# A recommender forward pass: the order of the last block, and a bias term fed through the contraction

## The chip, the cores and the metric

The kernel runs on one core of a Trainium2 chip. The metric is the device time of one execution in microseconds, shown as the median of three runs. A core has a matrix engine (TensorE, "PE" in the profile; its weight loads are shown as "PEld"), a vector engine (VectorE, "DVE"), a scalar engine (ScalarE, "ACT"), GpSimd ("POOL") and a sync engine (SyncE, "SP"). Each works through its own instructions in their order, and they wait for one another through semaphores. Data is worked on in SBUF (128 partitions); matmuls write into PSUM. Transfers from device memory are issued from an engine's queue; indirect ones (gathers by index) are issued by GpSimd, one instruction for 128 rows.

## The reference

For each of 16384 samples there are 69 user fields and one label, all of them indices into one table of 100001 rows of 96 floats. Every field's row `u` is weighed by an attention value from a small net on `[q, u, q - u, q * u]`, where `q` is the label's row; the weighed rows are summed in ten groups, and a three-layer net runs on the ten sums and `q`. Everything is float32.

```python
u = emb[batch_user]                              # (B, 69, 96)
ql = emb[batch_label[:, 0]]
z = concatenate([q, u, q - u, q * u], axis=-1)   # q: ql for each field
h = dice(z @ W1 + b1, a1)                        # 384 -> 64
att = (h @ W2 + b2) @ W3 + b3                    # 64 -> 16 -> 1
pre = where(batch_user < ITEM_NUM, u * att, 0)
x = concatenate([einsum('gf,bfe->bge', window, pre), ql])
h = dice(bn(x @ Wf1 + bf1), af1)                 # 1056 -> 200
h = dice(bn(h @ Wf2 + bf2), af2)                 # 200 -> 80
return h @ Wf3 + bf3
```

`dice(x, a)` is `(a * (1 - p) + p) * x` with `p = sigmoid(x)`. The groups hold 20, 20, 10, 10, 2, 2, 2, 1, 1 and 1 fields.

## The kernel before

**Tiling.** Samples come in 32 blocks of 512 (`BLK`). A block's 69 x 512 rows are cut into 69 chunks of 512 rows: 64 main chunks, each of 8 samples times the first 64 fields, and 5 single-field chunks, each one of the last five fields for all 512 samples. Two chunks make a pair `i`; there are 1104 pairs. `chunk(c)` (L232) says which chunk stands at place `c`; in the last block it puts the five single-field chunks after three quarters of the main ones.

**A pair's way.** `fetch(i)` (L299) issues eight gathers of 128 rows into `u` and turns each with a PE transpose into PSUM (`ptr`). From a half of it DVE makes `quT` (the rows times `q`) and then ACT `uT` (a copy). With `A = W1[1] - W1[2]`, `C = W1[0] + W1[2]`, and `Wp = W1[3]`, the first layer is `A.T uT + Wp.T quT + c`, where `c` (q through `C`, plus `b1`) is the same for all fields of a sample. `head_row(n)` (L252) makes `c` of a block. `seed(i)` (L276) opens the accumulation in PSUM with a bf16 matmul of zeros and lets ACT copy `c` into it, spread over the fields. `hidden(i)` (L323) adds the two products, each chunk into its own 64 of the 128 output partitions, and makes `y` by a sigmoid and a linear step on ACT and a product on DVE. `attend_rows` (L334) takes the attention values of four pairs, `spread` (L350) turns them and multiplies the group windows in (`rw`), and `pool(i)` (L367) sums a pair's rows into `pooled` with eight matmuls into the PSUM tile `acc` and a DVE copy. Single-field chunks go through `attend_tail` (L343) into `pres`. An fp32 matmul stands in the trace as two records, each with its weight load; these are called passes.

**Top net.** `top1` (L404), `top2` and `top3` run on a block's `pooled`, `qTs` and `pres`; `top_steps` (L439) cuts it into ten steps: eight quarter-parts of the two output halves of the first layer (together 16 matmuls for a half), then `top2`, then `top3`. `top3` writes each block's results out by an own transfer. `tail_weights` (L217) makes, early on, the weights of the single-field chunks on DVE.

**Order.** The order is written out by hand: the kernel turns the framework's scheduler off, and the loop at L481 puts, in step `i`, the stages of different pairs one behind the other: `seed(i-1)`, `pool(i-8)` (`POOL_LAG`), a band's `attend_rows`, `attend_tail(i-3)`, a band's `spread`, `hidden(i-2)`, `fetch(i)`, and then what `plan` holds for the step. That is the order in which each engine's queue gets its instructions. In the last fetching step four pools more are put ahead of the fetch (L503). The last block's top net runs in two halves of the samples, the first beside the last pairs, the second after the last pool.

**Buffers.** `u` has 14, `uT` and `quT` five, `y` eight; the indices of a block (`ids`) two. PSUM has two buffers each for transposes, `ph` and the small tiles, one for `acc` and one for the top net (`ps_m`).

**Start.** `ids` of block 0 is the first transfer on SP's queue; about twenty small transfers of weights follow on SP's and ACT's queues (L114 to L182).

Of the kernel before, what the change touches and what calls it, by code (L numbers as in the profile page):

```python
# [30 lines left out]
BF16 = mybir.dt.bfloat16  # L32
# [5 lines left out]
P = 128  # L38
# [6 lines left out]
BLK = 512  # L45
# [16 lines left out]
EARLY = 3 * NMAIN // 4  # L62
# [3 lines left out]
def rec_kernel(  # L66
# [5 lines left out]
    W1: bass.AP,  # L72
    b1: bass.AP,
    a1: bass.AP,
    W2T: bass.AP,
    b2: bass.AP,
    W3: bass.AP,
    b3: bass.AP,
    Wf1: bass.AP,
    bf1: bass.AP,  # L80
    af1: bass.AP,
    Wf2: bass.AP,
    bf2: bass.AP,
    af2: bass.AP,
    Wf3: bass.AP,
    bf3: bass.AP,
    wrow: bass.AP,
    wtile: bass.AP,
# [7 lines left out]
    tpool = ctx.enter_context(tc.tile_pool(name="tpool", bufs=5))  # L96
    hpool = ctx.enter_context(tc.tile_pool(name="hpool", bufs=3))
    ypool = ctx.enter_context(tc.tile_pool(name="ypool", bufs=8))
# [3 lines left out]

    def load_ids(n):
        ids = ipool.tile([P, NCOL], I32, tag="ids", name=f"ids{n}")
        nc.sync.dma_start(out=ids, in_=idx[n : n + 1].rearrange("o p n -> (o p) n"))
        return ids

    ids = {0: load_ids(0)}

# [4 lines left out]
    w1 = const.tile([E, 4, H1], F32, name="w1")  # L114
    nc.sync.dma_start(out=w1, in_=W1.rearrange("(k e) h -> e k h", e=E))
    Cq = const.tile([E + 1, 2, H1], F32, name="Cq")
    for i in range(2):
        nc.vector.tensor_add(Cq[0:E, i, :], w1[:, 0, :], w1[:, 2, :])
    nc.sync.dma_start(
        out=Cq[E : E + 1], in_=b1.rearrange("(o q h) -> o q h", o=1, q=1).to_broadcast([1, 2, H1])  # L120
    )
    Wp = w1[:, 3, :]
    A = const.tile([E, H1], F32, name="A")
    nc.vector.tensor_sub(A, w1[:, 1, :], w1[:, 2, :])

    qTs = []
    for i in range(2):
        t = const.tile([E + 1, BLK + NS], F32, name=f"qT{i}")
        nc.vector.memset(t[:, BLK:], 0.0)
        nc.vector.memset(t[E : E + 1, :], 1.0)  # L130
        qTs.append(t)

    def column(ap, name, n, copies=1):
        t = const.tile([n * copies, 1], F32, name=name)
        for i in range(copies):
            nc.sync.dma_start(out=t[i * n : (i + 1) * n, :], in_=ap.rearrange("(n o) -> n o", o=1))
        return t

    def one_minus(t, name):
        r = const.tile(list(t.shape), F32, name=name)  # L140
        nc.vector.tensor_scalar(r, t, -1.0, 1.0, ALU.mult, ALU.add)
        return r

    a1c = column(a1, "a1c", H1, 2)
    na1c = one_minus(a1c, "na1c")


    w2t = const.tile([H2, 2, H1], F32, name="w2t")
    for i in range(2):
        nc.sync.dma_start(out=w2t[:, i, :], in_=W2T)  # L150
    w3 = const.tile([H2, 1], F32, name="w3")
    nc.sync.dma_start(out=w3, in_=W3)
    w3b = const.tile([H2, E], F32, name="w3b")
    nc.vector.tensor_copy(w3b, w3.to_broadcast([H2, E]))
    b2c = column(b2, "b2c", H2)
    b2m = const.tile([H2, P], F32, name="b2m")
    nc.vector.tensor_copy(b2m, b2c.to_broadcast([H2, P]))
    b3r = const.tile([P, 1], F32, name="b3r")
    nc.sync.dma_start(out=b3r, in_=b3.rearrange("(o n) -> o n", o=1).to_broadcast([P, 1]))
# [6 lines left out]
    R = const.tile([P, 2 * G], F32, name="R")  # L166
    nc.scalar.dma_start(out=R, in_=wtile)
    wr = const.tile([E, NTAIL, G], F32, name="wr")
    nc.scalar.dma_start(out=wr, in_=wrow.rearrange("(o f) g -> o f g", o=1).to_broadcast([E, NTAIL, G]))


    wf1 = const.tile([E, G + 1, D1], F32, name="wf1")
    nc.scalar.dma_start(out=wf1, in_=Wf1.rearrange("(k e) n -> e k n", e=E))
    wf2 = const.tile([DH, 2, D2], F32, name="wf2")
    nc.scalar.dma_start(out=wf2, in_=Wf2.rearrange("(k e) n -> e k n", e=DH))
    wf3 = const.tile([D2, 1], F32, name="wf3")
    nc.scalar.dma_start(out=wf3, in_=Wf3)
    bf1c = [column(bf1[i * DH : (i + 1) * DH], f"bf1c{i}", DH) for i in range(2)]
    af1c = [column(af1[i * DH : (i + 1) * DH], f"af1c{i}", DH) for i in range(2)]
    bf2c = column(bf2, "bf2c", D2)  # L180
    af2c = column(af2, "af2c", D2)
    bf3c = column(bf3, "bf3c", 1)  # L182
# [11 lines left out]

    zrow = const.tile([1, 512], BF16, name="zrow")
    nc.vector.memset(zrow, 0.0)

    with tc.tile_pool(name="prep_ps", bufs=1, space=PSUM) as pps:
        pv = pps.tile([P, E], F32, name="pv")
        nc.tensor.matmul(pv, w2t.rearrange("a i h -> a (i h)"), w3b, start=True, stop=True)  # L200
        nc.vector.tensor_copy(vrep, pv)
        for i in range(2):
            nc.vector.tensor_copy(v2[i * H1 : (i + 1) * H1, i : i + 1], pv[i * H1 : (i + 1) * H1, 0:1])
        pb = pps.tile([P, 1], F32, name="pb")
        nc.tensor.matmul(pb, b2m, w3, start=True, stop=True)
        nc.vector.tensor_add(bb, pb, b3r)
# [25 lines left out]
    def chunk(c):  # L232

        n, k = divmod(c, NCH)
        if n == NBLK - 1 and k >= EARLY:
            k = NMAIN + k - EARLY if k < EARLY + NTAIL else k - NTAIL
        return n, k
# [14 lines left out]
    def head_row(n):  # L252

        cT = bpool.tile([P, BLK], F32, tag="cT", name=f"cT{n}")
        pc = ps_x.tile([P, BLK], F32, tag="x", name=f"pc{n}")
        for i in range(2):
            nc.tensor.matmul(
                pc[i * H1 : (i + 1) * H1, :],
                Cq[:, i, :],
                qTs[n % 2][:, i * NS : i * NS + BLK],  # L260
                start=True,
                stop=True,
            )
        nc.scalar.copy(cT, pc)

        cU = bpool.tile([P, BLK], F32, tag="cU", name=f"cU{n}")
        pc = ps_x.tile([P, BLK], F32, tag="x", name=f"pc2_{n}")
        nc.tensor.matmul(pc, Cq.rearrange("e i h -> e (i h)"), qTs[n % 2][:, 0:BLK], start=True, stop=True)  # L268
        nc.scalar.copy(cU, pc)
        return cT, cU  # L270

    def by_field(ap):

        return ap.rearrange("e (s o) -> e s o", o=1).to_broadcast([ap.shape[0], NS, FM])

    def seed(i):  # L276

        ph = ps_h.tile([P, 512], F32, tag="h", name=f"ph{i}")
        nc.tensor.matmul(ph, zrow[:, 0:P], zrow, start=True, stop=False)  # L279
        (n0, k0), (n1, k1) = chunk(2 * i), chunk(2 * i + 1)  # L280
        if n0 == n1 and k1 < NMAIN:
            nc.scalar.copy(  # L282
                ph.rearrange("h (s f) -> h s f", f=FM), by_field(cs[n0][0][:, k0 * NS : (k0 + 1) * NS])
            )
        elif n0 == n1 and k0 >= NMAIN and k1 >= NMAIN:
            nc.scalar.copy(ph, cs[n0][1])
        else:
            for j, (n, k) in enumerate([(n0, k0), (n1, k1)]):
                lo, hi = j * H1, (j + 1) * H1
                if k < NMAIN:  # L290
                    nc.scalar.copy(
                        ph[lo:hi].rearrange("h (s f) -> h s f", f=FM),
                        by_field(cs[n][1][lo:hi, k * NS : (k + 1) * NS]),
                    )
                else:
                    nc.scalar.copy(ph[lo:hi], cs[n][1][lo:hi, :])
        return ph

    def fetch(i):  # L299

        u = upool.tile([P, 8, E], F32, tag="u", name=f"u{i}")
        uT = tpool.tile([E, 2, 512], F32, tag="uT", name=f"uT{i}")
        quT = tpool.tile([E, 2, 512], F32, tag="quT", name=f"quT{i}")
        for j in range(2):
            n, k = chunk(2 * i + j)
# [14 lines left out]
            nc.scalar.copy(uT[:, j, :], ptr)  # L320
        return u, uT, quT

    def hidden(i, ph, uT, quT):  # L323

        for w, x, last in [(A, uT, False), (Wp, quT, True)]:
            for j in range(2):
                nc.tensor.matmul(ph[j * H1 : (j + 1) * H1, :], w, x[:, j, :], start=False, stop=last)  # L327
# [6 lines left out]
    def attend_rows(b, ys):  # L334

        pr = ps_x.tile([P, 512], F32, tag="x", name=f"prow{b}")
        for k, y in enumerate(ys):
            nc.tensor.matmul(pr[32 * k : 32 * (k + 1), :], v2, y, start=True, stop=True)  # L338
        row = rpool.tile([P, 512], F32, tag="row", name=f"row{b}")
        nc.scalar.copy(row, pr)  # L340
        return row

    def attend_tail(i, j, y, uT):  # L343
# [4 lines left out]
        nc.vector.scalar_tensor_tensor(pres[n][:, k - NMAIN, :], pa, bb[0:E], uT[:, j, :], ALU.add, ALU.mult)  # L348

    def spread(b, row):  # L350

        pt = ps_x.tile([P, 4, 4, 32], F32, tag="x", name=f"patt{b}")
        for t in range(4):
            nc.tensor.transpose(pt[:, t].rearrange("p k j -> p (k j)"), row[:, t * P : (t + 1) * P], ident)  # L354
# [100 lines left out]
    def at(step, work):  # L455
        plan.setdefault(step, []).append(work)
# [108 lines left out]
```

## Time and profile before

| | |
|---|---|
| median of three runs (lowest, highest) | 13356.97 us (13356.09, 13399.71) |
| the profiled execution | 11267.23 us |
| its span, first to last instruction | 11265.5 us |
| mean granted clock of the matrix engine | 0.707 of full speed |
| gathers | 8832 for `u`, 128 for `q` |
| last gather's end, from the span's start | 11196.0 us |

The profile is of one execution. Its page lists groups of instructions: line, engine, operation, what is written from what, shape and count, then busy time and mean ns of one, then the idle time of the engine just before them and what ended most of it. "issue" is time in which the engine waited for nothing that the profile shows. Matmuls are pipelined and their ends are modelled, so starts of neighbours tell more than durations. A timeline line has start, length, engine, line, operation and count. A row of the windows view has the stretch, its length, the busy time (and count) of PE, PEld, DVE, ACT and POOL, the granted clock, the share of the transfer engines and GB/s.

### The profile page before, as it was taken

To read this page: it belongs to the slowest core of one execution; us is meant where nothing else is said; L and a number is where in the kernel's file an instruction comes from. 1 tells how busy PE (TensorE), PEld (TensorE's weight loads), DVE (VectorE), ACT (ScalarE), POOL (GpSimd) and SP (SyncE) were. 2 spreads that over 40 slices of the span, in tenths; PEclk is the share of its full clock that TensorE was granted. 3 is DMA by queue.
4 is the path that set the end of the run, shared out by engine and by line. 5 is a ranking of instruction groups with operands and counts; after the bars stand their busy time and mean duration, and the time that the engine had idled before them with its cause. 6 is when DMAs were issued, how large, how long until landed. Compare 5 with 4: busy or idle time off the path is not lost.

```text
span 11265.5 us, 109062 instructions
## 1 busy us (share of the span) xinstructions
PE 9779.7 (87%) x41418; PEld 4767.8 (42%) x41418; DVE 3092.5 (27%) x5303; ACT 3770.0 (33%) x6092; POOL 8463.8 (75%) x8966
## 2 busy tenths in 40 slices
PE   7888888889888888888888888888888888888888
PEld 3444444444444444444444444444344444444444
DVE  3222222222222222222222222222222222222222
ACT  3333333333333333333333333333333333333333
POOL 7777777777777777777777777777777777777775
PEclk6767777676776777766767667776677776777767
DMA  2111111111111111111111111111111111111111
GB/s 44 41 41 41 40 41 40 41 40 41 40 41 40 41 40 40 40 41 40 41 40 41 40 41 41 40 40 41 40 41 40 41 41 41 41 40 40 41 40 31
DMA packets 295018, 453.66 MB, mean 40 GB/s; under 512 B 145953, under 2 KB 151107, under 8 KB 294498
## 3 DMA queue, kind: packets, MB, share of 16 engines
q0 software_dynamic: 286720, 440.98, 18.6%
q8 instruction: 332, 5.44, 0.2%
q1 hardware_dynamic: 6144, 4.77, 0.2%
q14 instruction: 188, 1.54, 0.0%
q10 hardware_dynamic: 1634, 0.94, 0.0%
HBM read 446.04 MB, written 0.07 MB: 40 GB/s over the span
## 4 chain that ended last, share of the span: by engine, by line
POOL 37%; PE 32%; issue 17%; DMA 11%; ACT 1%; DVE 1%; POOLq 0%
POOL u L225 36%; DMA u<-in_rows,ids 11%; PE ph L327 11%; PE acc L376 8%; PE p L413 3%; PE ptr L309 3%; PE prow L338 2%; PE ph L279 2%; POOL q L225 1%; PE pa L347 1%; ACT y L330 1%; PE patt L354 1%; DVE y L331 1%; ACT y L329 1%; PE pc L268 0%
## 5 line engine op out<-in xcount | busy, mean ns | idle before, releaser
L225 POOL DMA_INDIRECT u<-in_rows,ids x8832 | 8342.1, 945 | 2690.8 <-issue 2440.4
L309 PE MATMUL ptr<-ident,u 128*96 128x128 f32 x8832 | 2068.5, 357 | 1279.7 <-DMA u<-in_rows,ids 1256.1
L309 PEld LDWEIGHTS ptr<-ident,u 128*96 128x96 f32 x8832 | 1234.0, 156 | 3208.2 <-DMA u<-in_rows,ids 1641.4
L376 PEld LDWEIGHTS acc<-rw,u 128*96 128x96 f32 x16384 | 2064.6, 219 | 505.7 <-issue 501.0
L376 PE MATMUL acc<-rw,u 128*96 128x20 f32 x16384 | 2176.7, 283 | 3.7 <-DVE pooled L385 3.1
L320 ACT COPY uT<-ptr 96x512 f32<-96x512 f32 x2208 | 1285.1, 582 | 2305.9 <-DVE quT L312 2122.2
L331 DVE TENSOR_TENSOR y<-ph,y 128x512 f32<-128x512 f32 x1104 | 763.4, 692 | 4502.0 <-ACT y L330 4398.1
L329 ACT ACTIVATE y<-ph 128x512 f32<-128x512 f32 x1104 | 659.6, 598 | 3836.1 <-PE ph L327 3835.7
L327 PE MATMUL ph<-uT,A 96*64 96x512 f32 x4416 | 1801.1, 908 | 0.0
L327 PE MATMUL ph<-quT,w 96*64 96x512 f32 x4416 | 1686.1, 854 | 0.0
L312 DVE TENSOR_TENSOR quT<-ptr,qT 96x512 f32<-96x512 f32 x2048 | 1349.9, 679 | 683.1 <-PE ptr L309 678.5
L385 DVE COPY pooled<-acc 96x160 f32<-96x160 f32 x1008 | 432.8, 429 | 2262.8 <-PE acc L376 2262.3
L330 ACT ACTIVATE y<-y,a1c,na1c 128x512 f32<-128x512 f32 x1104 | 897.1, 813 | 37.2
L327 PEld LDWEIGHTS ph<-quT,w 96*64 96x64 f32 x4416 | 443.6, 194 | 1081.0 <-issue 1080.7
L282 ACT COPY ph<-cT 128x512 f32<-128x512 f32 x1008 | 591.1, 586 | 453.8 <-PE ph L279 451.6
L279 PE MATMUL ph<-zrow 1*128 1x512 bf16 x1104 | 527.6, 478 | 165.3 <-DVE y L331 163.1
L413 PE MATMUL p<-pooled,wf 96*100 96x512 f32 (+1 forms) x1320 | 651.7, 638 | 2.2 <-DVE x L400 1.7
L327 PEld LDWEIGHTS ph<-uT,A 96*64 96x64 f32 x4416 | 283.6, 177 | 555.3 <-issue 468.5
L338 PE MATMUL prow<-y,v 128*32 128x512 f32 x2208 | 452.2, 903 | 0.3 <-DVE y L331 0.3
L340 ACT COPY row<-prow 128x512 f32<-128x512 f32 x276 | 161.7, 586 | 643.8 <-PE prow L338 643.8
L413 PEld LDWEIGHTS p<-pooled,wf 96*100 96x100 f32 x1320 | 238.3, 189 | 272.6 <-issue 263.9
L413 PE MATMUL p<-pre,V 96*100 96x512 f32 (+1 forms) x660 | 310.9, 604 | 0.0
(67 smaller groups left out, 2359.6 us busy)
## 6 DMA issues: line engine op xcount, KB each, us to landing
u<-in_rows,ids POOLq DMA_INDIRECT x8832
ids<-in_idx SPq DMA_DIRECT2D x32, 140.0 KB
q<-in_emb,ids POOLq DMA_INDIRECT x128
wf<-in_Wf ACTq DMA_DIRECT2D x1, 825.0 KB
out<-res SPq DMA_DIRECT2D x31, 2.0 KB
w<-in_W SPq DMA_DIRECT2D x1, 96.0 KB
wf<-in_Wf ACTq DMA_DIRECT2D x1, 62.5 KB
a1c<-in_a SPq DMA_DIRECT2D x2, 0.2 KB
```

The source lines that it names most:

```text
L225: nc.gpsimd.indirect_dma_start(out=dst, out_offset=None, in_=table, in_offset=bass.IndirectOffsetOnAxis(ap=index, axis=0),)
L279: nc.tensor.matmul(ph, zrow[:, 0:P], zrow, start=True, stop=False)
L309: nc.tensor.transpose(ptr[:, t * P : (t + 1) * P], u[:, 4 * j + t, :], ident)
L312: nc.vector.tensor_tensor(quT[:, j, :].rearrange("e (s f) -> e s f", f=FM), ptr.rearrange("e (s f) -> e s f", f=FM), by_field(q[:, k * NS ...
L320: nc.scalar.copy(uT[:, j, :], ptr)
L327: nc.tensor.matmul(ph[j * H1 : (j + 1) * H1, :], w, x[:, j, :], start=False, stop=last)
L329: nc.scalar.activation(y, ph, AF.Sigmoid, scale=S_DICE)
L330: nc.scalar.activation(y, y, AF.Identity, bias=a1c, scale=na1c)
L331: nc.vector.tensor_mul(y, ph, y)
L338: nc.tensor.matmul(pr[32 * k : 32 * (k + 1), :], v2, y, start=True, stop=True)
L376: nc.tensor.matmul(pa[:, j, 2 * t : 2 * t + 2, :].rearrange("e n g -> e (n g)"), u[:, 4 * j + t, :], rw[:, 4 * t + i % 4, j, :], start=Tru ...
L413: nc.tensor.matmul(p1, w[:, h * DH : (h + 1) * DH], x, start=(k == 0), stop=(k == KTOP - 1))
```

## The change

**c through 32 contraction rows.** `seed`, the zero matmul and ACT's copy go. `uT` gets 128 partitions: rows 96 to 127 hold ones that pick one of 32 samples, one pattern for each `k % 4`, in twelve tiles that `ones()` fills once by DVE copies. The weights `As[n % 2]` hold, in rows 0 to 95, sixteen copies of `A`, and in rows 96 to 127 the block's `c` for 32 samples at a time; `head_rows` makes these with 16 small matmuls and two ACT copies. For single-field chunks one matmul with `Cq` on `qTs` opens the accumulation.

```diff
-    def seed(i):
-        ph = ps_h.tile([P, 512], F32, tag="h", name=f"ph{i}")
-        nc.tensor.matmul(ph, zrow[:, 0:P], zrow, start=True, stop=False)
...
+    def ones():
+        for i in range(3):
+            for v in range(4):
+                nc.vector.tensor_copy(
+                    uTs[v][i][E:P, :].rearrange("e (s f) -> e s f", f=FM),
+                    by_field(ident[E:P, E + v * NS : E + (v + 1) * NS]),
+                )
...
+    As = [const.tile([P, NMAIN // 4, H1], F32, name=f"A{i}") for i in range(2)]
+    nc.vector.tensor_sub(As[0][0:E, 0, :], w1[:, 1, :], w1[:, 2, :])
+    nc.vector.tensor_copy(As[0][0:E, 1:, :], As[0][0:E, 0:1, :].to_broadcast([E, NMAIN // 4 - 1, H1]))
+    nc.vector.tensor_copy(As[1][0:E], As[0][0:E])
...
+    def head_rows(n):
+        for h in range(2):
+            pc = ps_x.tile([P, NMAIN // 8, H1], F32, tag="x", name=f"pc{n}_{h}")
+            for k in range(NMAIN // 8):
+                x = (h * NMAIN // 8 + k) * 4 * NS
+                nc.tensor.matmul(pc[E:P, k, :], qTs[n % 2][:, x : x + 4 * NS], Cq, start=True, stop=True)
+            nc.scalar.copy(As[n % 2][E:P, h * NMAIN // 8 : (h + 1) * NMAIN // 8, :], pc[E:P])
...
+    def room(k):
+        v = k % 4 if k < NMAIN else turns.index(min(turns))
+        turns[v] += 1
+        return uTs[v][turns[v] % len(uTs[v])]
...
+    def hidden(i, uT, quT):
...
+            if k >= NMAIN:
+                nc.tensor.matmul(p, Cq, qTs[n % 2], start=True, stop=False)
...
+            if k < NMAIN:
+                nc.tensor.matmul(p, As[n % 2][:, k // 4, :], uT[j], start=True, stop=False)
+            else:
+                nc.tensor.matmul(p, A, uT[j][0:E], start=False, stop=False)
+        for j, p in enumerate(sums):
+            nc.tensor.matmul(p, Wp, quT[:, j, :], start=False, stop=True)
```

**Last block.** Its five single-field chunks come first. `top1` sums `pres` first, then `q`, then `pooled`. The top net runs in four quarters of 128 samples. In the last eight pairs (`CLOSE`, `c = NPAIR - 8`) the stages stand closer together: pools at a shorter lag, `hidden` between the two halves of a fetch, the last bands of two pairs instead of four.

```diff
-        if n == NBLK - 1 and k >= EARLY:
-            k = NMAIN + k - EARLY if k < EARLY + NTAIL else k - NTAIL
+        if n == NBLK - 1:
+            k = (k - NTAIL) % NCH
...
+    at(c + 5, rows_of(c, 4), spread_of(c, 4), pool_of(c), fetch_of(c + 5, [hidden_of(c + 4)]))
+    at(c + 6, pool_of(c + 1), pool_of(c + 2), fetch_of(c + 6, [hidden_of(c + 5)]))
+    at(c + 7, pool_of(c + 3), rows_of(c + 4, 2), fetch_of(c + 7, [spread_of(c + 4, 2), hidden_of(c + 6)]))
...
+    quarter = [top_steps(NBLK - 1, slice(r * P, (r + 1) * P)) for r in range(NQ)]
+    for s in range(10):
+        at(c - 4 + s // 3, quarter[0][s])
+        at(c + s // 3, quarter[1][s])
+    d = NPAIR
+    at(d, pool_of(c + 4), hidden_of(c + 7), pool_of(c + 5), *quarter[2][0:4], rows_of(c + 6, 2), *quarter[2][4:8])
+    at(d, quarter[2][8], spread_of(c + 6, 2), quarter[2][9], quarter[3][0])
+    at(d, pool_of(c + 6), pool_of(c + 7), lambda: store(B // P - 1), *quarter[3][1:])
```

**Output and weights.** `top3` now makes 128 results at a time as a column of a resident tile `res`; `store` turns its first 127 columns and writes them out in one transfer, and the last 128 results go out on their own (`top3_last`). The host packs all weights into two arrays, `near` and `far`, which are loaded by one transfer each, on SP's and ACT's queue, right after the first `ids`. Every block's `ids` is loaded 20 pairs ahead instead of 24. `quT` has four buffers and `y` six.

```diff
+    wn = const.tile([P, NEAR.width], F32, name="wn")
+    nc.sync.dma_start(out=wn, in_=near)
+    wf = const.tile([P, FAR.width], F32, name="wf")
+    nc.scalar.dma_start(out=wf, in_=far)
...
+    def store(n):
+        p4 = ps_x.tile([n, P], F32, tag="x", name="p4")
+        nc.tensor.transpose(p4, res[:, 0:n], ident)
+        r = ypool.tile([P, 512], F32, tag="y", name="r")[0:n, 0:P]
+        nc.vector.tensor_copy(r, p4)
+        nc.sync.dma_start(out=out[0 : n * P].rearrange("(m p) o -> m (p o)", p=P), in_=r)
```

## The prediction

> **What bounds the kernel.** I read the page's groups first, then POOL's waits, then the last 70 us of the timeline with the windows over the same stretch, and the start last. The page:
>
> ```profile
> span 11265.5 us, 109062 instructions
> ...
> PE 9779.7 (87%) x41418; PEld 4767.8 (42%) x41418; DVE 3092.5 (27%) x5303; ACT 3770.0 (33%) x6092; POOL 8463.8 (75%) x8966
> ...
> L225 POOL DMA_INDIRECT u<-in_rows,ids x8832 | 8342.1, 945 | 2690.8 <-issue 2440.4
> ...
> L309 PE MATMUL ptr<-ident,u 128*96 128x128 f32 x8832 | 2068.5, 357 | 1279.7 <-DMA u<-in_rows,ids 1256.1
> ...
> L279 PE MATMUL ph<-zrow 1*128 1x512 bf16 x1104 | 527.6, 478 | 165.3 <-DVE y L331 163.1
> ```
>
> PE has the largest busy share, yet it sits 1256 us before the transposes, waiting for gathers. POOL's 75% is misleading: (8342.1 + 2690.8) / 8832 = 1.249 us from one gather to the next, and POOL's waits say that the 0.30 us between two is its own issue:
>
> ```profile
> POOL u L225 <- issue: 2440.4, 8010, 0.3
> POOL u L225 <- DMA u<-in_rows,ids: 117.6, 386, 0.3
> POOL u L225 <- PE ptr L309: 109.1, 358, 0.3
> ...
> POOL q L225 <- DMA ids<-in_idx: 2.1, 1, 2.1
> ```
>
> Whatever is named, no wait of a u gather is over 0.3 us: POOL is never held by a full buffer. The sum is therefore: first gather at 3.4 us, (8832 + 128) x 1.249 = 11,192 us of gathers, last one ending at 11,196.0, and 69.5 us of tail. The change keeps all 8960 gathers, so **only the start, the pace of a gather and the tail can move the span**. The tail:
>
> ```profile
> 11195.04 0.94 POOL L225 DMA_INDIRECT u<-in_rows,ids  x1 [0.30 <-issue]
> 11195.84 2.75 PE L376 MATMUL acc<-rw,u 128*96 128x20 f32 x16
> ...
> 11208.22 1.92 PE L309 MATMUL ptr<-ident,u 128*96 128x128 f32 x8
> ...
> 11236.14 7.98 PE L413 MATMUL p<-pooled,wf 96*100 96x256 f32 x20 [0.51 <-DVE pooled L385]
> ...
> 11248.42 6.25 PE L413 MATMUL p<-pooled,wf 96*100 96x256 f32 x20 [1.72 <-DVE x L400]
> ...
> 11262.83 0.47 DVE L432 TENSOR_SCALAR res<-p,bf3c 1x256 f32<-1x256 f32 x1 [1.11 <-PE p L430]
> ```
>
> The last data is transposed 12 us after its gather, because four pools stand before it on PE. Four more pools stand behind the last pair (11,224 to 11,236). Then a half block goes through the top net in two column halves, 10.6 and 8.9 us to their last matmul. The windows give the clock there:
>
> ```profile
> 11196.00:11208.20 12.20, 10.66 (x64) 10.31 (x65) 1.96 (x4) 1.37 (x2) 0.00 (x0) 0.50 0.03 5
> 11208.20:11224.30 16.10, 14.82 (x61) 7.19 (x60) 5.22 (x10) 7.19 (x12) 0.00 (x0) 0.87 0.00 0
> 11224.30:11236.10 11.80, 9.78 (x64) 9.34 (x64) 2.09 (x5) 0.00 (x0) 0.00 (x0) 0.57 0.01 1
> 11236.10:11265.50 29.40, 21.51 (x70) 14.13 (x70) 1.92 (x4) 3.22 (x6) 0.00 (x0) 0.73 0.00 0
> ```
>
> The third figure from the end of a row is the granted clock; weighted, 0.69.
>
> **Profile and median.** The profiled run is 11,267 us, the median 13,357: 1.186 times as long. I can't see why in one trace. [...] I take it that the shown runs are paced by the same gathers, 13,357 / 11,265 slower, and scale my sum by 1.186.
>
> **Part by part.** *c through the contraction.* Removed per pair: the bf16 zero matmul (527.6 us in all) and ACT's seed copy (L282, 591 us). The A matmuls take 128 rows instead of 96; an fp32 pass over 512 columns has 429 ns between starts at 96 rows (L413) and 433 at 128 (L338), so nothing is added. Single-field chunks gain a Cq matmul: 160 x 2 records at L257's 0.43 us = 136 us; head_row's three wide matmuls (109 us) become 512 small ones, 1024 records bounded by 0 and by the L376 price of 0.13 us = 136 us (taken: they load 32 columns, L376 96). PE net: -364 us busy, 3.7%. All of it, and ACT's, lies under the gathers: **worth 0** while they pace. Fewer buffers (quT 5 to 4, y 8 to 6, u unchanged at 14) hold no gather, since only u is written by them, and a pair's u is released at a lag of 8 pairs.
>
> *Packed weights.* Some twenty small loads become two. ids still goes first on SP, but the 1.2 MB load now starts on ACT's queue at once, where R (10 KB) and wr went first. The ids packets ran from 1.77 to 2.71 us; if each engine's eight alternate with rows of 9.7 KB (16 KB instruction packets took 1.0 us, so some 0.4 us each), the first gather is late by 0 to 3 us; I take 1. Later readiness of weights is covered by the 14 u buffers, some 100 us of gathers.
>
> *ones() and As*, DVE copies from SBUF to SBUF. [...] The row: while L220's ten-operation chain ran in SBUF (41 to 45 us), three gathers took 1.07 instead of 0.94 us, 0.13 for each 1.37 us. Some 8 us of copies (12 of 512 and 2 of about 1000 columns, at 0.5 and 1 us from L385's and L250's per-column rates) would cost 0.8 us so. [...] Start in all: **+2.5 us (0 to +11)**.
>
> *Order in the last block.* Its 32 main pairs now come last, 16 samples each, so a quarter of 128 samples is complete after every eight pairs. Quarters 0 and 1 run beside the gathers, quarter 2 fills PE's waits after the last one, and only quarter 3 depends on the last pair. The new tail along PE, from the last gather's end, at full / half clock. Prices: a 128-column pass 110 / 214 ns (starts of L309's neighbours; 100 weight columns here, 96 there), eight acc matmuls 1.5 / 2.75 us, A to sigmoid 2.0 / 3.7 (11,213.3 to 11,215.3, and 11,192.2 to 11,196.0); dice on 128 columns 1.8 with PE's wait (L398, L399, L400 taken down from 512 and 256 columns).
> - Landing 1.6 (early gathers: end 18.24, transposed 19.81), transposes, quT and uT 1.8, one pool below these; hidden begins at 3.5 / 4.6, ends for PE at 5.4 / 8.2.
> - Pool and quarter 2's first half (32 passes): 10.4 / 17.9; y is ready well before (2.2 us after sigmoid's start). Rows 1.1 / 2.0, second half 3.5 / 6.9: 15.0 / 26.8.
> - top2 with its dice, spread, top3, first part of quarter 3: 20.7 / 33.8.
> - Two pools with the 0.5 us accumulator wait, store's transpose: 24.7 / 40.4.
> - Quarter 3: 24 passes, dice, 32 passes: 32.7 / 54.3. Dice, top2, dice, top3, add 0.35, output 2.2 (11,263.3 to 11,265.5): **39.8 / 61.9**.
>
> Written as 17.7 + 22.1 / clock, the clock 0.69 seen in the old tail gives 49.6. [...] PE was busy for 10.66 of 12.20 us and stayed at 0.50. I take 49.6, that is -20. The big store of 127 rows goes out before quarter 3's passes, 13 us or more of cover; uncovered it would cost its landing, a few us.
>
> Sum in the profile: 11,265.5 + 2.5 - 20 = **11,248**. Scaled: 13,357 - 17.5 x 1.186 = **13,336 us**, -0.16%.
>
> **Rivals.**
> 1. *PE paces the shown runs.* Busy 9780 at clock 0.707 would be up to 13,830 at a clock held at 0.5, around the median. Then -3.7%: 12,860. Against it: all 401 rises of the clock in the trace follow windows with PE 99.8% busy on the mean, falls follow windows at 60%; a PE that never waits wouldn't be kept at half. Nothing says that unprofiled runs differ in this, so it stays open.
> 2. *PE comes late to the last gather* (slower). Quarters 0 and 1 put 128 passes and their ends on PE in the steps from twelve to five pairs before the end. At half clock: 30 us, three extra pools 8, two bands 7, less eight steps of 1.2 us slack (10.0 - a bare pair of 9.3 - 0.5 for the zero matmul, 11,078.8 to 11,088.1) = some 36 us, and the last four pairs don't win it back. Then +36 - 20 + 2.5 = +18.5, scaled 13,379. It decides from 17.5 us of lateness. Against it: the clock rose for 27 us when the old kernel crowded its first half in there, and PE was on time at 11,196.
> 3. *It doesn't shorten the tail* (half clock throughout, long start): -7.6 + 11: 13,361.
>
> **Numbers.** About 0.5% (67 us) is what a measurement of this kernel can tell from no change. Main case 0.68 (13,310 to 13,360), rival 2 0.10 and rival 3 0.04, rival 1 with partial forms 0.18. The highest of three earlier runs, 13,400, lies 43 above the median, so the range goes to 13,410; downward to 13,240, which takes the mildest of rival 1. Faster 0.20; within 0.5% 0.74; slower 0.06 (rival 2 with noise, or a pace raised by over 7.5 ns a gather).
>
> **What would show it.** 1.249 us a gather and no POOL wait over 0.3; last gather's end within 0 to 11 us of 11,196; the last transposes within 3 us of landing; a tail near 50 us with quarter 3's passes at 0.11 to 0.21 us[...]. The forecast is wrong if the pace of gathers moves, or if the median falls by over 2% while the profile falls by under 0.5%: then PE paces the runs shown.

## The result, and the profile after

The changed kernel took 13,214.26 us (median of four runs, 13,198.27 to 13,222.82), the kernel before 13,378.34 us (four runs, 13,356.09 to 13,427.98): a ratio of 0.9871, with an interval of 0.9838 to 0.9904. The forecast was 13,336 us with a range down to 13,240, so the change brought more than the range held.

One thing has to be known to read the profiles: that of the kernel before was of an execution of 11,267 us, 16% shorter than any of its timed runs, while that of the changed kernel is of one of the timed kind, 13,198 us. The two pages can't be subtracted. The page of the changed kernel shows its span, the busy time by engine, the shares of the chain that ended last, and four groups (busy us and mean ns of one, then the idle time just before them).

```profile
span 13196.5 us, 108603 instructions
...
PE 8794.3 (67%) x41797; PEld 4570.3 (35%) x41797; DVE 3032.1 (23%) x5324; ACT 3167.2 (24%) x4969; POOL 8455.0 (64%) x8966
...
PE 55%; issue 19%; another core or an unknown queue 16%; POOL 3%; ACT 3%; DVE 3%; DMA 1%; DVEq 0%; POOLq 0%
...
L249 POOL DMA_INDIRECT u<-in_rows,ids x8832 | 8333.3, 944 | 4574.9 <-issue 2366.2
L389 PE MATMUL acc<-rw,u 128*96 128x20 f32 x16384 | 1934.7, 260 | 1825.7 <-issue 1468.4
...
L305 PE MATMUL ptr<-ident,u 128*96 128x128 f32 x8832 | 1607.8, 318 | 1428.3 <-issue 1111.7
...
L336 ACT ACTIVATE y<-ph 128x512 f32<-128x512 f32 x1104 | 659.5, 597 | 5154.5 <-remote 2718.6
```

A gather takes 944 ns here, 945 in the first profile: it isn't longer. But POOL's idle time is 4575 us, not 2691, and PE stands idle before the transposes and the pools for nothing that the profile names ("issue"), not for a gather. POOL's waits (total us, times, longest us) show the reverse of the first profile, where none of a `u` gather was over 0.3 us:

```profile
POOL u L249 <- issue: 2366.2, 7748, 1.8
POOL u L249 <- remote: 967.1, 316, 7.3
POOL u L249 <- PE acc L389: 557.5, 127, 38.1
POOL u L249 <- PE ptr L305: 441.7, 227, 5.8
```

The last three hold POOL for 1966 us, up to 38 us at a time. "Remote" is a wait whose releasing signal the trace doesn't hold; the other two are waits for PE's pools and transposes, so the `u` buffers are full and the gathers wait for PE. The last transposes start at 13,149.5, 75 us behind the end of the last gather (13,074.9). **PE paces this execution.**

### The profile page after: what moved, and what is told of

It reads as the page before. It is cut to its first block, busy times and chain, and to the rows that moved or that the text cites. A ratio compares the mean times of both kernels' runs of the same rounds, so it can differ in the third digit from the quotient of the medians.

```text
span 13196.5 us, 108603 instructions
## 1 busy us (share of the span) xinstructions
PE 8794.3 (67%) x41797; PEld 4570.3 (35%) x41797; DVE 3032.1 (23%) x5324; ACT 3167.2 (24%) x4969; POOL 8455.0 (64%) x8966
## 4 chain that ended last, share of the span: by engine, by line
PE 55%; issue 19%; another core or an unknown queue 16%; POOL 3%; ACT 3%; DVE 3%; DMA 1%; DVEq 0%; POOLq 0%
PE acc L389 11%; PE ptr L305 10%; PE ph L330 9%; PE ph L334 9%; PE p L428 7%; PE prow L345 4%; POOL u L249 3%; PE patt L362 1%; DVE quT L308 1%; PE pa L354 1%; ACT uT L317 1%; ACT y L337 1%; PE ph L327 1%; PE pc L282 1%
## 5 line engine op out<-in xcount | busy, mean ns | idle before, releaser
L389 PE MATMUL acc<-rw,u 128*96 128x20 f32 x16384 | 1934.7, 260 | 1825.7 <-issue 1468.4
L305 PE MATMUL ptr<-ident,u 128*96 128x128 f32 x8832 | 1607.8, 318 | 1428.3 <-issue 1111.7
L334 PE MATMUL ph<-quT,wn 96*64 96x512 f32 x4416 | 1692.6, 745 | 178.2 <-issue 168.5
L330 PE MATMUL ph<-uT,A 128*64 128x512 f32 x4096 | 1633.2, 800 | 140.7 <-issue 136.2
L337 ACT ACTIVATE y<-y,wn,na1c 128x512 f32<-128x512 f32 x1104 | 897.6, 813 | 36.7
L334 PEld LDWEIGHTS ph<-quT,wn 96*64 96x64 f32 x4416 | 446.6, 172 | 1225.4 <-issue 1223.3
L345 PE MATMUL prow<-y,v 128*32 128x512 f32 x2208 | 634.2, 792 | 246.1 <-issue 143.8
L330 PEld LDWEIGHTS ph<-uT,A 128*64 128x64 f32 x4096 | 280.7, 161 | 678.3 <-issue 659.4
L362 PE MATMUL patt<-ident,row 128*128 128x128 f32 x1108 | 247.5, 343 | 253.5 <-issue 167.4
L367 DVE SCALAR_TENSOR_TENSOR rw<-patt,bb,wn 128x320 f32<-128x320 f32 x554 | 273.6, 534 | 146.2 <-remote 84.2
```

Of the source, the lines that this page charges most:

```text
L305: nc.tensor.transpose(ptr[:, t * P : (t + 1) * P], u[:, 4 * j + t, :], ident)
L330: nc.tensor.matmul(p, As[n % 2][:, k // 4, :], uT[j], start=True, stop=False)
L334: nc.tensor.matmul(p, Wp, quT[:, j, :], start=False, stop=True)
L337: nc.scalar.activation(y, y, AF.Identity, bias=a1c, scale=na1c)
L345: nc.tensor.matmul(pr[32 * k : 32 * (k + 1), :], v2, ys[b + k], start=True, stop=True)
L389: nc.tensor.matmul(pa[:, j, 2 * t : 2 * t + 2, :].rearrange("e n g -> e (n g)"), u[:, 4 * j + t, :], rw[:, t, j, :], start=True, stop=True,)
```

## The experiments

The times of one group of runs are compared with the kernel before on the same chip. e1 to e8 ran on one chip, in two groups; e9 to e11, e12 to e15 and e16 to e18 on three others.

### The kernel before, profiled again

No edit.

> The kernel before, unchanged, for a profile taken where the times are taken. Theory A (PE paces the shown runs, held up by something that the granted clock does not show): a span near 13,350 us, each gather still 0.94 us long and 1.25 us apart when POOL is free, POOL waiting some 2,000 us for pools and transposes, transposes 50 us or more behind their gathers, and transposes 0.7 and 1.4 us apart in places, as in the trace of after. Theory B (slow gathers, what the prediction assumed): gathers 1.1 us or longer and 1.48 us apart throughout, PE close behind them. If the span is 11,265 us again, a profiled execution differs from a timed one and both fall.

Measured: 13,530.83 us, among eleven timed runs with a median of 13,534.62. The page's groups:

```profile
span 13529.1 us, 109062 instructions
...
PE 9996.0 (74%) x41418; PEld 5009.6 (37%) x41418; DVE 3076.3 (23%) x5303; ACT 3743.1 (28%) x6092; POOL 8476.0 (63%) x8966
...
L225 POOL DMA_INDIRECT u<-in_rows,ids x8832 | 8354.1, 946 | 4893.6 <-issue 2203.1
L376 PEld LDWEIGHTS acc<-rw,u 128*96 128x96 f32 x16384 | 2129.0, 225 | 2851.1 <-issue 2845.0
L279 PE MATMUL ph<-zrow 1*128 1x512 bf16 x1104 | 521.7, 473 | 2696.1 <-DVE y L331 1777.0
```

At this length the kernel before has the shape of the changed one: gathers of 946 ns, POOL idle for 4894 us, and the last transposes 61 us behind the last gather's end. So theory A holds, and theory B (longer gathers) falls. The zero matmul waits 2696 us, 1777 of them for `y` of three pairs earlier; the first profile had 165 us in that row. A stretch of the timeline (start, length, engine, line, operation; in brackets the idle time before it) shows what PE does there:

```profile
5098.71 0.37 PE L309 MATMUL ptr<-ident,u 128*96 128x128 f32 x1 [3.12 <-issue]
...
5100.11 0.37 PE L309 MATMUL ptr<-ident,u 128*96 128x128 f32 x1 [1.03 <-issue]
...
5101.51 0.16 PEld L309 LDWEIGHTS ptr<-ident,u 128*96 128x96 f32 x1 [2.64 <-issue]
...
5102.92 0.37 PE L309 MATMUL ptr<-ident,u 128*96 128x128 f32 x1 [2.44 <-issue]
...
5104.31 0.10 PEld L279 LDWEIGHTS <-zrow 1*128 1x128 bf16 x1 [2.64 <-issue]
...
5113.43 0.42 DVE L385 COPY pooled<-acc 96x160 f32<-96x160 f32 x1 [30.92 <-remote]
5113.66 0.95 POOL L225 DMA_INDIRECT u<-in_rows,ids  x1 [4.95 <-remote]
...
5115.57 0.59 ACT L340 COPY row<-prow 128x512 f32<-128x512 f32 x1 [31.74 <-remote]
...
5118.47 0.60 ACT L329 ACTIVATE y<-ph 128x512 f32<-128x512 f32 x1 [2.32 <-remote]
...
5120.69 0.58 PE L279 MATMUL ph<-zrow 1*128 1x512 bf16 x1 [17.40 <-issue]
```

Transposes and their loads start 1.40 us apart here, though the gathers of these rows had been issued some 70 us before; in most of this trace a transpose starts 0.11 or 0.21 us behind the last. Then DVE and ACT stand for 31 us, waiting for sums whose matmuls PE had begun before 5090 (the last of the `quT` products of L327, which ACT reads at 5118.47, began at 5087.25). PE in turn waits for `y` behind them. So PE, ACT and DVE stand together. POOL does not: its gathers go on every 1.25 us until 5107.76, and then it waits 4.95 us. Counted over the trace, PE (weight loads included) has 314 pauses of over 3 us between two starts, 2339 us in all; 276 of them, 1995 us, lie before the zero matmul. The first profile has none, and its span is 2264 us shorter. **What sets the two executions apart is these pauses**, not longer gathers. The two sums needn't agree so closely, since PE also waited for gathers in the first profile.

### c alone, and the order alone

The first is the kernel before with the change's `uTs`, `ones`, `As`, `head_rows` and `hidden`, and nothing else of it:

```diff
-                phs[i - 1] = seed(i - 1)
...
-                ys[i - 2] = hidden(i - 2, phs.pop(i - 2), *hs[i - 2])
+                ys[i - 2] = hidden(i - 2, *hs[i - 2])
```

The second is the changed kernel with the zero matmul, ACT's copy and the old `hidden` put back:

```diff
+            if i >= 1:
+                phs[i - 1] = seed(i - 1)
...
-        return lambda: ys.__setitem__(k, hidden(k, *hs[k]))
+        return lambda: ys.__setitem__(k, hidden(k, phs.pop(k), *hs[k]))
```

> The kernel before with c brought in through the 32 contraction rows alone; order of the last block, weights, output as before. Theory A (the work taken from PE is what gained): most of the change's 1.3%, that is 0.8 to 1.3% under the kernel before. Theory C (the last block's order gained, through a mechanism that the prediction missed): under 0.3%. [...]

> The changed kernel with the zero matmul and the scalar engine's copy of c put back; the new order, packed weights and the output in one transfer stay. Theory A: the tail's 20 to 40 us alone, 0.1 to 0.3% under the kernel before. Theory C: about 1% or more under it.

Measured: c alone 13,247.02 us, ratio 0.9784 (0.9765 to 0.9803); the order alone 13,596.49 us, 1.0043 (1.0026 to 1.0060). **All of the gain is c's, and the rest of the change costs**: what e3 keeps is the new order, but also the packed weights, the new way out and the fewer buffers. The starts of the transposes of pairs 140 and 1000 in the traces tell where in the span:

| kernel | us per pair, 140 to 1000 | from pair 1000 to the end |
|---|---|---|
| before (e1) | 12.108 | 1306.2 |
| c alone (e2) | 11.856 | 1257.7 |
| order alone (e3) | 12.143 | 1360.1 |
| changed, first profile and e8 | 11.801, 11.795 | 1272.2, 1294.1 |
| before, first profile | 10.135 | 1108.8 |
| changed, e12 | 10.133 | 1096.6 |

0.252 us a pair over 1104 pairs is 278 of the 284 us between the spans of e1 and e2: the gain is spread evenly. Of the 84 us between the spans of e3 and e1, 54 lie behind the start of pair 1000, which takes in the last block. The tail behind the last gather is 118.0 us in e1, 148.8 in e3.

The pages of e1 and e2 also tell what became of the zero matmul's wait. Lines of e2:

```profile
PE 8828.9 (67%) x41466; PEld 4528.4 (34%) x41466; DVE 3052.7 (23%) x5316; ACT 3160.1 (24%) x4956; POOL 8454.4 (64%) x8966
...
L370 PE MATMUL acc<-rw,u 128*96 128x20 f32 x16384 | 1916.4, 261 | 1523.6 <-issue 1242.5
L292 PE MATMUL ptr<-ident,u 128*96 128x128 f32 x8832 | 1648.5, 320 | 1783.8 <-issue 1283.5
```

PE is busy for 1167 us less than in e1, at a granted clock of 0.734 in place of 0.673, and idle for 883 us more; 284 us are left. Before the pools and the transposes it stood 4 and 392 us in e1, and stands 1524 and 1784 here. The pauses of over 3 us are 321 in number and 2159 us in sum, so they did not go with the zero matmul: most of them moved to other instructions.

### Zero weights

```diff
-    Wp = w1[:, 3, :]
+    Wp = const.tile([E, H1], F32, name="Wz")
+    nc.vector.memset(Wp, 0.0)
...
-    nc.vector.tensor_sub(As[0][0:E, 0, :], w1[:, 1, :], w1[:, 2, :])
+    nc.vector.memset(As[0][0:E, 0, :], 0.0)
```

> The changed kernel with A and Wp set to zero: it leaves out what u and q*u give to the first layer; every instruction, count and shape stays. If the hidden hold-up of PE comes from the current that the array draws (theory A1): clearly faster than the changed kernel, 5 to 15%, towards the 11,250 us of the gathers, with fewer transposes 0.7 and 1.4 us apart. If it comes from instructions, semaphores or fetches (theory A2): the changed kernel's 13,214 us within 0.5%.

Measured: 13,280.34 us, 0.9808 (0.9788 to 0.9829), with 295 pauses and a granted clock of 0.734; the changed kernel itself has 295 pauses and 0.733. Zero weights in the first layer make no difference to them: theory A1, which had the time fall by 5 to 15%, falls.

### More records, fewer records, less work

e1 to e4 fitted a theory R: time in proportion to the number of instructions and semaphore updates, as though recording them set the pace. Three edits were made against it, with the changed kernel beside them. To the kernel before, memsets on DVE that nothing waits for:

```diff
+                for _ in range(4):
+                    nc.vector.memset(spare, 0.0)
```

> Edit: the kernel before, and behind each copy to uT four DVE memsets of one column, 8 a pair, 8832 in all, that wait for nothing new and free nothing. Theory R (in the timed runs the time goes with the number of instructions plus engine semaphore updates, about 9.84 of them per us, whatever they do): 133,139 + 8,832 = 141,971, so a ratio of 1.066 and some 14,430 us. Theory P (PE's own matmuls, and its waits for y, set the time): DVE is busy for about a quarter of the span, so 8 short instructions a pair delay PE little: ratio 0.998 to 1.010.

To c alone, ACT's linear step folded into DVE's:

```diff
-        nc.scalar.activation(y, y, AF.Identity, bias=a1c, scale=na1c)
-        nc.vector.tensor_mul(y, ph, y)
+        nc.vector.scalar_tensor_tensor(y, y, ra1c, ph, ALU.add, ALU.mult)
```

> Edit: c through the 32 rows alone (as in e2), and the linear step on ACT folded away: y = (sigmoid + a/(1-a)) x in one DVE operation, the factor 1-a goes into the weights of the next layer. It takes 1104 ACT instructions and as many updates away. Theory R: 130,469 - 2,208 = 128,261 against 133,139: ratio 0.963, some 1.7 per cent below e2. Theory P with the wait for y: e2 has no matmul left that waits for y before its time, so the shorter way to y frees nothing: ratio 0.978, within 0.3 per cent of e2.

To the kernel before, the first layer on half of the columns:

```diff
-                nc.tensor.matmul(ph[j * H1 : (j + 1) * H1, :], w, x[:, j, :], start=False, stop=last)
+                nc.tensor.matmul(ph[j * H1 : (j + 1) * H1, 0:256], w, x[:, j, 0:256], start=False, stop=last)
```

> Edit: the kernel before, with the four fp32 matmuls of the first layer of each pair on 256 of 512 columns (this leaves out half of the first layer's u and q*u terms, the number of instructions and of updates stays). Theory R: no change, 0.997 to 1.003. Theory P: 8 passes of 256 columns less, 0.11 us each at full clock and 0.21 at half, 0.9 to 1.7 us a pair of some 12.1: ratio 0.86 to 0.93 if PE's work sets the pace, 0.95 if half of it is hidden.

> The changed kernel unaltered, beside e5 to e7 and the kernel before on one chip. Theory R: 131,062 against 133,139: ratio 0.984, behind e2 (0.978) by 0.6 per cent. Theory P (the new order is worth nothing, c is worth 2.2 per cent): 0.978 to 0.982, the same as e2. Both expect it slower than e6 if e6 is faster than e2.

Measured, beside a kernel before of 13,394.13 us:

| run | us | ratio (interval) | theory R | theory P |
|---|---|---|---|---|
| e5 | 13,562.66 | 1.0132 (1.0104 to 1.0160) | 1.066 | 0.998 to 1.010 |
| e6 | 13,144.71 | 0.9814 (0.9801 to 0.9828) | 0.963 | 0.978 |
| e7 | 13,295.82 | 0.9928 (0.9912 to 0.9943) | 1.000 | 0.86 to 0.95 |
| e8 | 13,199.85 | 0.9846 (0.9833 to 0.9860) | 0.984 | 0.978 to 0.982 |

**R falls** by e5 and e6; that it met e8 was chance. **P, PE's work, falls as well**, by e7, and e5 and e8 lie just above its ranges. The page of e7 (busy us, then the groups as above) shows where the saved work went:

```profile
PE 9124.6 (69%) x41418; PEld 5372.9 (40%) x41418; DVE 3087.8 (23%) x5303; ACT 3739.5 (28%) x6092; POOL 8475.7 (64%) x8966
...
L279 PE MATMUL ph<-zrow 1*128 1x512 bf16 x1104 | 565.0, 512 | 2875.5 <-DVE y L331 2118.2
```

PE is busy for 871 us less than in e1 (9996; e1 is of the other group), but the granted clock fell from 0.673 to 0.618, the zero matmul waits 179 us longer, and there are 389 pauses of 2513 us in place of 314 of 2339. Most of what PE saves, it stands. The fold of e6 takes a handover out of the way to `y`, and brought nothing beyond c that these two groups can tell (0.9784 in the one, 0.9814 in the other). e6 is yet the fastest of the kernels tried on this chip, 0.4% under e8, whose interval its own doesn't touch.

### Three edits that met another chip

Theories W and S ask what in c gives its gain (the wait for `y` of the zero matmul, or its work and signals), N whether the number of PE's instructions sets the pace. All three edits are of the kernel before:

```diff
-                phs[i - 1] = seed(i - 1)
+                phs[i - 2] = seed(i - 2)
```

```diff
+        for _ in range(4):
+            nc.tensor.matmul(ph[:, 0:8], zrow[:, 0:P], zrow[:, 0:8], start=False, stop=False)
```

```diff
-            for t in range(4):
+            for t in range(2):
                 nc.tensor.matmul(
-                    pa[:, j, 2 * t : 2 * t + 2, :].rearrange("e n g -> e (n g)"),
-                    u[:, 4 * j + t, :],
-                    rw[:, 4 * t + i % 4, j, :],
+                    pa[:, j, 4 * t : 4 * t + 4, :].rearrange("e n g -> e (n g)"),
+                    u[:, 4 * j + 2 * t, :],
+                    rw[:, 8 * t + i % 4 : 8 * t + i % 4 + 5 : 4, j, :],
```

> Edit: the kernel before, with seed(i-1) of each step replaced by seed(i-2): the zero matmul then needs the PSUM buffer of pair i-4, whose y was made a step earlier, in place of that of pair i-3, whose y comes from matmuls only one step old. The same instructions, the same updates, PE's work unchanged. Theory W (the gain of c is the wait for y that goes: 1777 us of PE idle were put down to it in the repeat of before, 165 in the first profile): ratio 0.975 to 0.985, as with c alone. Theory S (the gain is the work and the signals of the zero matmul and of ACT's copy): 0.997 to 1.003. Worse than 1.003 would mean that PE now waits for ACT's copy of c, which is one step younger.

> Edit: the kernel before, with four more zero matmuls of 8 columns behind each zero matmul (they add nothing to the sum): 4416 matmuls and 4416 weight loads more, 8832 PE instructions on 82,836. Theory N (in the timed runs PE gets through a nearly fixed number of instructions per us, 6.1 to 6.3 in all eight runs so far, whatever their size): 82,836 + 8,832 = 91,668 at 6.15 to 6.3 per us, a ratio of 1.07 to 1.10. Theory W or S: the columns cost 0.06 us a matmul and load, 0.26 us a pair, of which e7 says that a sixth to a whole shows: 1.003 to 1.025.

> Edit: the kernel before, with four pool matmuls of 40 columns a pair in place of eight of 20 (this leaves half of the rows out of the group sums): 8192 passes and as many weight loads less, a fifth of PE's instructions, and 0.7 us a pair of its work at full clock, 1.3 at half. No update goes. Theory N: 66,452 instructions at 6.15 to 6.3 per us is under 10,800 us, so the gathers would be the bound: 11,250 to 11,500 us, ratio 0.84 to 0.86. Theory W or S: as much work less as in e7, which gave 0.993: 0.985 to 0.995.

Measured: 1.0002 (0.9993 to 1.0010), 0.9998 (0.9989 to 1.0006) and 0.9991 (0.9983 to 1.0000), but beside a kernel before of **11,262.68 us in all of its 33 runs (11,257.17 to 11,270.53)**. Here the timed runs are what the first profile was of, and a tenth of PE's instructions more, or a fifth fewer, is worth nothing. The three ratios say nothing of the other chip.

### The changed kernel there

> The changed kernel unaltered. Where the kernel before runs near 13,400 us beside it: 0.982 to 0.990, as twice before. Where it runs near 11,260 us the gathers pace both, and the prediction's own sum holds: 11,265.5 + 2.5 - 20, a ratio of 0.997 to 0.9995; a theory that the gain belongs to the kernel whatever paces it says 0.987 there too.

> As e9. Near 13,400 us: theory W (the wait for y) 0.975 to 0.985, theory S (work and signals of the zero matmul and of ACT's copy) 0.997 to 1.003. Near 11,260 us: 1.000 again, which tells nothing new.

> As e10. Near 13,400 us: theory N (PE gets through 6.1 to 6.3 instructions per us, whatever their size) 1.07 to 1.10, theories W and S 1.003 to 1.025. Near 11,260 us: 1.000 again.

> As e11 (half of the rows left out of the group sums). Near 13,400 us: theory N 0.84 to 0.86, theories W and S 0.985 to 0.995. Near 11,260 us: 0.999 again.

Measured on a third chip, beside 11,260.24 us: the changed kernel 11,253.40 us, **0.9994 (0.9986 to 1.0003)**; the others 1.0003 (0.9994 to 1.0011), 1.0000 (0.9992 to 1.0009) and 0.9990 (0.9981 to 0.9999). The page of the changed kernel there, chain and two groups:

```profile
POOL 46%; DMA 21%; issue 17%; PE 16%; ACT 0%; DVE 0%; POOLq 0%
...
L249 POOL DMA_INDIRECT u<-in_rows,ids x8832 | 8335.5, 944 | 2691.6 <-issue 2332.0
L305 PE MATMUL ptr<-ident,u 128*96 128x128 f32 x8832 | 2040.4, 327 | 2157.9 <-DMA u<-in_rows,ids 2134.6
```

Gathers and their transfers are two thirds of the chain; PE waits 2135 us for them before the transposes, where the kernel before waited 1256: the time that c saves PE (busy 9024 us, 755 less than in the first profile of before) comes out as waiting. The tail is 57.6 us, in this one trace. Kernels with the old last block had 64.4 to 76.9 in six traces (e9, e10, e13, e14, e16, e17) and 69.5 in the first profile; with half of the pool matmuls the old block had 56.7, 67.9 and 56.3 (e11, e15, e18). Windows of the new tail (stretch, length, busy us and count of PE, PEld, DVE, ACT and POOL, granted clock, share of the transfer engines, GB/s):

```profile
11193.80:11206.00 12.20, 12.10 (x89) 7.42 (x90) 4.63 (x10) 5.15 (x9) 0.00 (x0) 1.00 0.01 4
11206.00:11220.00 14.00, 12.38 (x92) 9.03 (x90) 2.38 (x6) 3.96 (x8) 0.00 (x0) 1.00 0.00 1
11220.00:11235.00 15.00, 12.42 (x69) 11.93 (x70) 2.51 (x8) 1.19 (x3) 0.00 (x0) 0.62 0.01 4
11235.00:11251.40 16.40, 9.60 (x46) 8.31 (x44) 1.39 (x4) 2.57 (x6) 0.00 (x0) 0.60 0.00 1
```

PE has hardly a gap in the first stretch (busy for 12.10 of 12.20 us), because it is behind. Its timeline:

```profile
11203.76 0.64 PE L305 MATMUL ptr<-ident,u 128*96 128x128 f32 x4
...
11205.63 1.07 PE L330 MATMUL ph<-uT,A 128*64 128x512 f32 x2
...
11224.98 2.74 PEld L389 LDWEIGHTS acc<-rw,u 128*96 128x96 f32 x16
```

The last transposes start 10.0 us after the last gather's end (11,193.8). The three edits of the kernel before once more, on a fourth chip, which was of this kind too:

> As e9 and e13, for a kernel before near 13,400 us. Theory W (the wait for y) 0.975 to 0.985, theory S (work and signals of the zero matmul and of ACT's copy) 0.997 to 1.003. With the kernel before near 11,260 us: 1.000, a third time.

> As e10 and e14, for a kernel before near 13,400 us. Theory N (PE gets through 6.1 to 6.3 instructions per us) 1.07 to 1.10, theories W and S 1.003 to 1.025. With the kernel before near 11,260 us: 1.000, a third time.

> As e11 and e15 (half of the rows left out of the group sums), for a kernel before near 13,400 us. Theory N 0.84 to 0.86, theories W and S 0.985 to 0.995. With the kernel before near 11,260 us: 0.999, a third time.

Measured, beside 11,258.80 us: 1.0002 (0.9993 to 1.0011), 1.0000 (0.9991 to 1.0009) and 0.9993 (0.9985 to 1.0002). W, S and N stay untried where they matter.

## Why the prediction was wrong

**The step that failed is "Profile and median".** It took the shown runs to be "paced by the same gathers, 13,357 / 11,265 slower" and scaled the sum by 1.186. That was an estimate from the two times alone, and no trace supported it: in the runs of that length a gather is 943 to 946 ns, not 1.186 times 945. They are paced by PE with its pauses (314 in e1, 2339 us), and POOL waits for it. All that followed for the shown runs was worked out for another bound. That they got faster, as forecast, is luck: the forecast's gain was to come from the tail, and without c the change was 0.4% slower (e3).

**c, "worth 0 while they pace".** The condition was right and so, as far as is shown, is the number under it: 0.9994 for the whole change in e12, with PE's saving turned into waits for gathers (c alone wasn't run there). Where PE paces, c alone gave 0.9784. The saving forecast for PE was 364 us busy; e12 has 755 less, and at a clock of 0.752 in place of 0.707.

**Rival 1, PE paces the shown runs.** That was the case, at a third to two fifths of its price: -3.7% forecast, -1.3% and -1.5% measured. The price came from busy time, and little of that lies on the path: e2 took 1167 us of it away and its span is 284 us shorter, e7 took 871 away and gained 98. The reason given against the rival (a PE that never waits wouldn't be kept at half clock) didn't touch it, since this PE is idle for 3533 us of e1, at a clock of 0.673. Its test pointed the right way, the median moves and the profile of the other kind does not, but the 2% that it asked for was reached by c alone (2.2%) and not by the whole change.

**Start, +2.5.** The first gather came at 6.98 us in e12 (6.96 in the first profile of the changed kernel) instead of 3.4: 3.6 us where I took 1, just over the 0 to 3 given. The twelve copies of `ones()` took 4.28 us in e12, and the three gathers beside them 1.16, 1.09 and 1.09 us instead of 0.94, 0.5 us in all. Of the 2.5 us, the 1.5 for the copies was my estimate, and so was the upper end of 11; no run shows either. The row's 0.8 us would have been enough. Sum: +4.1, and the last gather ends 4.3 to 4.6 us later than in e13 to e15 on the same chip.

**Tail, -20.** It was -12 where it can be seen (57.6 in e12 against 69.5 in the first profile; 64.4 and 71.9 in e14 and e13 on the chip of e12). Rival 2 had the missing part: PE comes 8 us late to the last data (transposed 10.0 us after the last gather's end, not 1.6), where its price was 36 at half clock and the clock was full. Set against the forecast's own steps, hidden ends at 15.3 instead of 5.4; from there on each step takes what it was given, at full clock as far as the first part of quarter 3 (15.9 us for 15.3) and near half clock afterwards (26.4 us for 19.1 at full and 28.1 at half). The clock was not 0.69 throughout: 1.00 for the first 30 us, and 0.50 in the 20 us from 11,223.7 on, behind 3.4 us in which PE was busy for 1.61. On the chip of e3 there was no gain in the tail at all: the last transposes start 61 us behind the last gather's end in e1, and 91 in e3.

**The sum where the gathers pace**: +4.1 - 12 = -8, forecast -17.5, measured -6.8 us in the medians, with 1 inside the interval of the ratio: it can't be told from no change.

**Still open.** What makes the pauses on the one chip, and what in c shortens the time there. R and P are refuted in the forms given, zero weights don't matter (e4), and N can't carry the gain, since c alone has 96 PE instructions more than before (82,932 against 82,836) and takes 2.2% less. The row of the zero matmul (2696 us idle, 1777 for `y`) speaks for W less than it seems to: the matmul went, and PE's idle time rose by 883 us. The edit that takes this wait away alone never ran there. Nor is it shown that the pauses belong to the kernel's own running: every timed run on record has a span and a granted clock, so it seems that all were recorded, and none without recording stands beside them.

## What to carry to other kernels

When a profile's span is 16% below every timed run, it isn't a profile of what was timed: take one more of the kernel before, on the chip that the times come from, before any sum is scaled. Where one engine paces, look at whom the waits of the others go to, not at its busy time. A kernel whose consumer lags by all of its buffers gained here from c, which takes work and a wait out of the consumer, and nothing from a rearranged tail; and no row of waits told how much, since a wait that is taken away can come back before the next instruction (in e2 the zero matmul's 2696 us went, and PE was idle for 883 us more). Work out how late the engine behind the pacing one is at the last transfer before rearranging what follows it.

## What the runs showed of the hardware

- The kernel before stands at 11,255 to 11,271 us in 103 runs on three chips, and at 13,359 to 13,571 us in 20 runs on another, where the median moved by 1% between two groups of runs.
- In the nine traces of 13,155 to 13,613 us PE's starts pause for over 3 us 294 to 389 times in an execution (2.1 to 2.6 ms in all), the longest for 25 to 55 us; in the eleven of about 11,260 us there are at most three such pauses, none over 3.7 us. In all the long traces records of signals are missing: e1 holds 10,646 of PE's 13,219 semaphore updates, 3,406 of ACT's 6,090, and 37,277 from transfers, where the first profile holds 13,215, 6,092 (two more than the instructions name) and 144,125. e12 lacks 14 of PE's. Missing records and pauses go together here, but whether one causes the other no run shows, and 8832 more instructions (e5) cost 1.3% only.
- 4416 extra matmuls of 8 columns with their loads, or 8192 passes fewer, moved the time by at most 0.1% where the gathers pace.
